# The last convolution on 32x32 tiles of the array

## The chip, the cores and the metric

The kernel runs on one core of one Trainium2 chip. The metric is the device time of one execution in microseconds; a lower time is better. Before the change it is 6811.06 us (median of three runs, 6808.49 to 6813.17).

## What is computed

The input is eight images of 16 channels and 256 x 256 pixels in f32. Four layers follow one another, each of the form "normalise, convolve, add":

```
x = x + L0(gn(x))     # capsule convolution with routing
x = x + L1(gn(x))     # spline (KAN) convolution, 3x3
x = x + L2(gn(x))     # attention over 16x16 patches, each channel for itself
x = x + L3(gn(x))     # 3x3 convolution, 16 -> 16 channels, through the FFT
```

`gn` subtracts the mean and divides by the standard deviation of a group of two channels of one image. L3 multiplies the spectra of the padded kernel and of the image, which is a circular 3x3 convolution: an output pixel needs the nine pixels around it, and rows and columns wrap at the borders of the image. The addition of x and the normalisation are linear for given statistics, so the kernel folds both into the weights of L3: the weights are scaled by 1/std of the input channel, an identity is added to the middle tap, and the mean becomes a bias for each output channel.

## The kernel before, in words

The layers run one after the other; each leaves its result in DRAM. The change touches the end of layer 2 and all of layer 3.

Layer 2 (`layer2`, `attend`) works through 8 images x 16 channels, one call of `attend` for each. A call normalises the patches on VectorE (DVE, L1411), adds the embedding on GpSimd (POOL, L1415), forms the products of the attention on TensorE (PE, L1421 to L1448), and adds the residual on DVE (L1452): `y` holds 256 rows as 128 partitions x 2 rows. Its statistics go into `st3` (L1460, L1461), and two DMAs on the queue of SyncE (SP) write the rows to `x3` (L1464). `x3` is [H + 4, 16 channels, 256] for each image, with the first row kept for row -1 and the last three for rows 256 to 258; the nested function `wrap` copies these four rows from DRAM to DRAM with two DMAs (L1363, L1364), for an image at the third channel of the next one, for the last image at the start of layer 3. A scheduler places the instructions of all engines but SP, whose order in this layer is that of the code. At channel 6 of the last image `first3` loads two of the four pieces of image 0 into the patch buffer `pt0`, which is free by then (L1388).

Layer 3 (`layer3`) keeps the order of the code on all engines. Eight input rows by 16 channels fill the 128 partitions, and six output rows come of them, in three pairs. `fetch3` loads 11 such groups, each starting six rows after the one before, as 128 partitions x 11 rows of 1 KB in one DMA (L1474), and two GpSimd copies fill the wrapped columns (L1478, L1479). An image has four such pieces. `step` (called for three values of s) makes four column tiles at once: three row pairs of piece s and one of the last piece. A product is 128 partitions by 32 outputs (2 rows x 16 channels) by 512 columns (two groups); the three horizontal taps accumulate in PSUM `p3s` (L1532). DVE adds the bias and moves the sums to `y3` (L1544), and eight DMAs on the queue of ScalarE (ACT) write a step's `y3` to the output (L1551). `weights` makes the scaled weights of the next image on DVE (L1511). The statistics of the last image are not ready when the layer begins; their steps stand in the list `todo` (`stats3_steps`), and one of them is put behind the products of each group pair, with a PSUM buffer `p3b` of their own.

Every DMA of SP and ACT is given the next of eight semaphores in turn, and waits before its issue until the DMA that used the semaphore last has landed.

Of the kernel before, what the change touches and what calls it, by code (L numbers as in the profile page):

```python
# [18 lines left out]
P = 128  # L19
# [6 lines left out]

R3 = 6
# [81 lines left out]
def _ident3():  # L109

    a = np.zeros((R3 + 2, C, 3, R3 // 2, C, 2), np.float32)
    for c in range(C):
        for r in range(R3):
            a[r + 1, c, 1, r // 2, c, r % 2] = 1.0
    return a.reshape(P, 3 * C * R3)

# [15 lines left out]
def _layout(w0, bw, sw, sc, bias, wq, bq, wk, bk, wv, bv, w3):  # L132
# [28 lines left out]

    l3 = np.zeros((R3 + 2, C, 3, R3 // 2, C, 2), np.float32)
    for dh in range(3):
        for dw in range(3):
            for ro in range(R3):
                l3[ro + dh, :, dw, ro // 2, :, ro % 2] = w3[:, :, 2 - dh, 2 - dw].T
    l3 = l3.reshape(P, 3 * C * R3)
# [110 lines left out]
class _Net:  # L278
    def __init__(self, ctx, tc, d, out):
# [19 lines left out]
        self.x3 = [self.dram.tile([H + 4, C, W], F32, name=f"x3_{b}") for b in range(B)]  # L299
# [929 lines left out]
    def stats3_steps(self, pool, name, bank):  # L1229
# [31 lines left out]
        def sums():  # L1261

            for q in range(4):
                for dw in range(3):
                    nc.tensor.matmul(z()[32 * q : 32 * q + 32, :8], self.w3[:, dw, 0], nm, start=dw == 0, stop=dw == 2)
# [33 lines left out]
    def early3(self, pool):  # L1299

        self.st3 = pool.tile([P, P, 6], F32, name="st3"), pool.tile([P, 2, P], F32, name="mv3")
        self.nc.vector.memset(self.st3[1], 0.0)
        self.w3 = pool.tile([P, 3, R3 // 2, 32], F32, name="w3")
        self.nc.sync.dma_start(out=self.w3.rearrange("p d t m -> p (d t m)"), in_=self.d["l3"])
        self.small = pool
# [8 lines left out]
    def layer2(self, images=range(B), channels=range(C)):  # L1314
# [3 lines left out]
        with ExitStack() as st:  # L1318
# [43 lines left out]
            def wrap(b):  # L1362
                nc.sync.dma_start(out=self.x3[b][0:1], in_=self.x3[b][H : H + 1])  # L1363
                nc.sync.dma_start(out=self.x3[b][H + 1 : H + 4], in_=self.x3[b][1:4])  # L1364


            pts, ress = {images[0]: self.pt[images[0] % 2]}, {(images[0], 0): first}
            with tc.manual_schedule(engines={mybir.EngineType.SP}):
                for n, b in enumerate(images):
                    after = images[n + 1] if n + 1 < len(images) else None  # L1370
                    for c in channels:
                        if c == 1:
                            ress[b, 1] = rows(b, 8)
                        if c == 2 and n:
                            wrap(images[n - 1])
# [16 lines left out]
                self.wrap = lambda: wrap(images[-1])  # L1392

    def first3(self, b):

        self.x3s = {}
        at = self.pt[0].rearrange("p h c r f -> p (h c r f)")
        for i, n in enumerate((R3 // 2, 0)):
            xs = at[:, i * 4096 : i * 4096 + 11 * WP].rearrange("p (g w) -> p g w", w=WP)
            self.x3s[n] = self.fetch3(b, n, xs)  # L1400
# [7 lines left out]
    def attend(self, mid, psum, b, c, pt, res, emb, wqk, wv, bqk, bv, bc, stats):  # L1408
# [37 lines left out]
        for o in range(2):  # L1446
# [4 lines left out]
        y = mid.tile([P, 2, 16, 16], F32, name="y2", bufs=3)  # L1451
        nc.vector.tensor_tensor(  # L1452
            y,
# [4 lines left out]
        y = y.rearrange("p o n j -> p o (n j)")  # L1458
        i = b * C + c
        nc.vector.bn_stats(stats[0][:, i, :], y.rearrange("p o w -> p (o w)"))  # L1460
        nc.vector.bn_aggr(stats[1][:, :, i], stats[0][:, i])  # L1461
        rows = self.x3[b][1 : 1 + H, c].rearrange("(h k r) w -> k r h w", k=2, r=8)
        for k in range(2):
            nc.sync.dma_start(out=rows[k], in_=y[:, k])  # L1464
# [3 lines left out]
    def fetch3(self, b, n, xs):  # L1468

        nc = self.nc  # L1470
        G = 11
        g0, k = n * G, min(G, -(-H // R3) - n * G)
        at = self.x3[b][g0 * R3, 0]
        nc.sync.dma_start(  # L1474
            out=xs[:, :k, 1 : 1 + W],
            in_=bass.AP(tensor=at.tensor, offset=at.offset, ap=[[W, P], [R3 * C * W, k], [1, W]]),
        )
        nc.gpsimd.tensor_copy(xs[:, :k, 0:1], xs[:, :k, W : W + 1])  # L1478
        nc.gpsimd.tensor_copy(xs[:, :k, WP - 1 : WP], xs[:, :k, 1:2])  # L1479
        return xs  # L1480

    def layer3(self, images=range(B)):
# [6 lines left out]
        groups, G, T = -(-H // R3), 11, R3 // 2  # L1489
        with ExitStack() as st:  # L1490
            io = st.enter_context(tc.tile_pool(name="l3_io", bufs=4))
            psum = st.enter_context(tc.tile_pool(name="l3_ps", bufs=6, space=PSUM))
            w = self.w3
            stat = dict.fromkeys(images, self.bc3)

            def bank():
                t = []

                def get():
                    if not t:  # L1500
                        t.append(psum.tile([P, 512], F32, name="p3b", tag="p3b", bufs=1))
                    return t[0]
# [3 lines left out]
            def fetch(b, n):  # L1506
                return self.fetch3(b, n, io.tile([P, G, WP], F32, name="x3s", bufs=8))

            def weights(b):
                ws = io.tile([P, 3, T, 32], F32, name="ws3", bufs=2)  # L1510
                nc.vector.scalar_tensor_tensor(  # L1511
                    ws.rearrange("p d t m -> p (d t m)"),
                    w.rearrange("p d t m -> p (d t m)"),
# [7 lines left out]
            def step(b, s, ws, xs):  # L1521

                work = [(t, s, xs[s]) for t in range(T)] + [(s, T, xs[T])]
                n = [min(G, -(-(H - 2 * t) // R3) - q * G) for t, q, _ in work]
                y = io.tile([P, G, W], F32, name="y3", bufs=3)
                for g in range(0, max(n), 2):
                    ps = psum.tile([P, 2, W], F32, name="p3s")
                    size = [min(2, k - g) for k in n]
                    for dw in range(3):
                        for q, (t, _, x) in enumerate(work):  # L1530
                            if size[q] > 0:
                                nc.tensor.matmul(  # L1532
                                    ps[32 * q : 32 * q + 32, : size[q]],
                                    ws[:, dw, t],
# [121 lines left out]
```

## Time and profile before

The profiled execution is one of its own. Times in us; shares are of the span.

| | |
|---|---|
| median of three runs | 6811.06 |
| span of the profiled execution | 6812.0 |
| first product of layer 3, start | 6449.8 |
| last product of layer 3, start | 6802.0 |
| PE busy, share | 6236.7, 92% |
| DVE busy, share | 5454.4, 80% |
| POOL busy, share | 3189.4, 47% |
| ACT busy, share | 2697.8, 40% |
| DMA packets, bytes | 451064, 811.67 MB |

The parts that the text uses are these. The page's rows of busy tenths cut the span in 40 slices; layer 3 is the last two, layer 2 about the six before them. In a line of the groups, `out<-in` are tiles of the program, `128*32` the part of the array that a product uses (rows by columns), then the shapes, the count, the busy time and the mean duration, and the idle time before the group with what ended it. In the timeline a line is a run of alike instructions: start, length, engine, line of the code, count. `PEld` is PE's loading of weights, `SPq` and `ACTq` the issue of DMAs by those engines. In the windows the busy times of the engines in a stretch of time stand side by side, then the granted clock of TensorE, the busy share of the 16 DMA engines and the bytes moved.

### The profile page before, as it was taken

The page shows a single profiled execution, that of the slowest core. Times are in us where ns is not written, and L with a number is a line of the kernel's source. Part 1 is how long each engine was busy: PE and PEld are TensorE (multiplying, and loading weights), DVE is VectorE, ACT ScalarE, POOL GpSimd, SP SyncE. Part 2 cuts the span into 40 slices and gives each one's busy share as a digit, 9 for nine tenths or more (in the row PEclk, how much of TensorE's full clock was granted, in tenths as well). Part 3 has the DMA queues.
Part 4 walks back from the last instruction along what each step waited for, and adds up shares of the span by engine and source line. Part 5 has one row for each costly group of instructions (what it writes and reads, how often), then busy time and mean ns, then how long its engine had stood idle before and what let it go on. Part 6 is the DMA issues. An engine that isn't in the chain of part 4 may idle for free. (4 is left out here: it accounts for less than half of the span.)

```text
span 6812.0 us, 105519 instructions
## 1 busy us (share of the span) xinstructions
PE 6236.7 (92%) x43144; PEld 2778.8 (41%) x43144; DVE 5454.4 (80%) x6462; ACT 2697.8 (40%) x3834; POOL 3189.4 (47%) x1885
## 2 busy tenths in 40 slices
PE   3899889899888998989986999999999999999999
PEld 1333333333333333333332444444444666666633
DVE  5799999999999999999997999999999433333322
ACT  1333333333333333333332888888888222112100
POOL 0566666666666666666666344444443111111100
PEclk9999999999999999999996999999999999999999
DMA  6233333333333333333332555555556434332376
GB/s 256 60 86 95 94 87 93 93 87 87 87 87 87 93 93 90 91 90 91 87 87 72 184 174 176 176 175 175 175 177 188 121 93 102 83 93 80 98 225 181
DMA packets 451064, 811.67 MB, mean 119 GB/s; under 512 B 57490, under 2 KB 299282, under 8 KB 415378
## 3 DMA queue, kind: packets, MB, share of 16 engines
q1 hardware_dynamic: 380946, 737.52, 36.6%
q10 hardware_dynamic: 69632, 67.39, 3.4%
q8 instruction: 339, 5.55, 0.3%
q14 instruction: 147, 1.20, 0.1%
HBM read 594.31 MB, written 211.03 MB: 118 GB/s over the span
## 5 line engine op out<-in xcount | busy, mean ns | idle before, releaser
L744 POOL TENSOR_TENSOR dd<-dd 128x1024 f32<-128x1024 f32 x512 | 1213.8, 2371 | 617.6 <-DVE dd L735 597.5
L1000 PE MATMUL ps<-bases,tw 128*32 128x512 f32 (+1 forms) x13824 | 1361.2, 546 | 16.1 <-POOL bases L969 6.6
L735 DVE SCALAR_TENSOR_TENSOR dd<-rb,v 128x1024 f32<-128x1024 f32 (+1 forms) x1024 | 1066.9, 1083 | 98.6 <-PE rb L724 93.1
L969 POOL TENSOR_TENSOR bases<-e,a 128x1024 f32<-128x1024 f32 (+1 forms) x264 | 621.5, 2377 | 927.6 <-DVE e L967 927.3
L623 DVE TENSOR_TENSOR pr<-v,fb 128x2048 f32<-128x2048 f32 (+1 forms) x512 | 1011.5, 2017 | 24.2 <-PE pl L633 12.8
L517 PE MATMUL cv<-kt,w 128*128 128x512 f32 x2048 | 1000.5, 611 | 27.7 <-DVE dd L735 21.5
L526 ACT COPY v<-cv 128x1024 f32<-128x1024 f32 x512 | 517.1, 1010 | 1152.4 <-PE cv L521 1152.4
L1000 PEld LDWEIGHTS ps<-bases,tw 128*32 128x32 f32 x13824 | 596.2, 109 | 802.5 <-issue 484.8
L744 POOL TENSOR_TENSOR s<-s,dd 128x512 f32<-128x512 f32 x512 | 670.5, 1310 | 35.1
L724 PE MATMUL rb<-rs,ct_fold 32*128 32x512 f32 x3584 | 609.5, 650 | 71.3 <-ACT rs L706 67.9
L633 PE MATMUL pl<-pr,ct_fold 128*32 128x512 f32 x3584 | 533.1, 607 | 120.2 <-DVE pr L623 120.2
L744 POOL TENSOR_TENSOR s<-v,dd 128x512 f32<-128x512 f32 x256 | 330.0, 1289 | 664.9 <-DVE dd L735 664.9
L1415 POOL TENSOR_TENSOR t<-t,emb 128x512 f32<-128x512 f32 x128 | 162.0, 1266 | 962.1 <-DVE t L1411 948.2
L521 PE MATMUL cv<-kt,w 64*128 64x512 f32 x2048 | 579.0, 641 | 0.0
L517 PEld LDWEIGHTS cv<-kt,w 128*128 128x128 f32 x2048 | 354.6, 190 | 525.5 <-issue 300.5
L1421 PE MATMUL pqk<-w_qk,t 128*128 128x512 f32 x1024 | 483.5, 595 | 4.6 <-POOL t L1415 4.6
L1432 ACT ACTIVATE vt<-pv,w_b2v 128x128 f32<-128x128 f32 x512 | 146.1, 367 | 842.3 <-PE pv L1428 842.3
L1452 DVE TENSOR_TENSOR y<-po,res 128x512 f32<-128x512 f32 x128 | 88.5, 691 | 486.8 <-PE po L1448 486.8
L977 DVE SCALAR_TENSOR_TENSOR bases<-xr,xm,bases 128x1024 f32<-128x1024 f32 (+1 forms) x264 | 447.7, 1734 | 0.3 <-POOL bases L969 0.3
L954 ACT ACTIVATE sq<-a 128x1024 f32<-128x1024 f32 (+1 forms) x264 | 263.7, 999 | 231.3 <-DVE a L946 230.5
L724 PEld LDWEIGHTS rb<-rs,ct_fold 32*128 32x128 f32 x3584 | 173.2, 185 | 415.3 <-issue 220.8
L1532 PE MATMUL p3s<-x3s,ws 128*32 128x512 f32 (+1 forms) x3114 | 327.5, 561 | 4.5 <-issue 4.5
(255 smaller groups left out, 8493.3 us busy)
## 6 DMA issues: line engine op xcount, KB each, us to landing
kt<-d SPq DMA_DIRECT2D x256, 516.0 KB
xr<-x1p SPq DMA_DIRECT2D x120, 1024.0 KB
d<-dn ACTq DMA_DIRECT2D x64, 516.0 KB
xs<-in_x_dram SPq DMA_DIRECT2D x16, 2048.0 KB
xs<-in_x_dram SPq DMA_DIRECT2D x64, 512.0 KB
res<-in_x_dram SPq DMA_DIRECT2D x64, 512.0 KB
x<-s SPq DMA_DIRECT2D x128, 256.0 KB
x1p<-s SPq DMA_DIRECT2D x128, 256.0 KB
```

The costliest lines, as they stand in the source:

```text
L517: nc.tensor.matmul(ps()[:, n], w[:, 0, j, :], t[:, a : a + 2, 0:W], start=True, stop=False)
L521: nc.tensor.matmul(ps()[:, n], w[at, 1, j, :], t[at, a : a + 2, 2 - n : 2 - n + W], start=False, stop=True)
L526: nc.scalar.copy(v[h]()[:, 4 * g : 4 * g + 4, j * W : j * W + W], ps().rearrange("p n (a w) -> p (n a) w", w=W),)
L623: nc.vector.tensor_tensor(pr()[:, :n].rearrange("p n (r w) -> p n r w", w=W), v[h]()[:, 4 * g : 4 * g + n].rearrange("p n (r w) -> p n r w ...
L633: nc.tensor.matmul(pl()[at : at + 32], sel[:, g, h, :], pr()[:, t, :], start=h == 0 and g == 0, stop=h == 1 and (g == 1 or t == 3),)
L724: nc.tensor.matmul(r()[:, n], spread[at, g, h, :], rs()[at], start=True, stop=True)
L735: nc.vector.scalar_tensor_tensor(dd()[:, :n], r()[:, :n], 1.0 / B, v[h]()[:, a : a + n], ALU.subtract, ALU.mult)
L744: op("POOL", us, lambda: nc.gpsimd.tensor_tensor(out[0](), a[0](), b[0](), ALU.add), a[1] + b[1], out[1])
L969: nc.gpsimd.tensor_tensor(ring[n % 3][:, 0, p : p + m, 1 : 1 + W], rows(e), rows(a), ALU.subtract)
L977: nc.vector.scalar_tensor_tensor(r, rows(part[1]), xm[:, b : b + 1], v, ALU.is_gt, ALU.mult)
L1000: nc.tensor.matmul(out if k is None else out[:, k], lhs, rhs, start=start, stop=stop, skip_group_check=True)
L1421: nc.tensor.matmul(ps, t[:, n, k * P : (k + 1) * P], wqk[:, n, :], start=n == 0, stop=n == 1)
```

## The change

`x3` becomes [8, 16 channels, 16, 2, 258] for each image: the row modulo 8 comes first, and a row carries its wrapped columns. In `attend`, `y` has room for these two columns, two POOL copies fill them, and one DMA writes both rows of all partitions. `wrap` is gone.

In layer 3 a partition is (row mod 8, channel), and the 33 groups of 8 rows (the last is a copy of the first pair of rows) follow one another with no row loaded twice. A group of 32 partitions is a pair of rows by 16 channels. A product takes 32 partitions by 32 outputs by 512 columns, and two pairs of input rows (q = 0 and 1) x three taps make one pair of output rows. For a strip `s` of 64 output rows, the four row groups of the array write four banks of a PSUM tile and the four column groups are four runs of 16 rows; there are two such tiles, `p3`, which fill PSUM. As q = 0 and q = 1 write a bank from different row groups, ACT copies a few elements (`seen`) between them. ACT adds the bias for two banks, DVE for the other two, and the eight stores of a strip are divided between the queues of SP and ACT. Image 0 has 24 of its groups loaded in layer 2; the other nine, and three groups that the boundary between the two loads cuts, are loaded at the start of layer 3, followed by images 1 and 2. Image n + 2 is loaded after the first half of image n. The steps of the last image's statistics take a whole `p3` tile and are placed at the end of half images. The core of the diff:

```diff
-        self.x3 = [self.dram.tile([H + 4, C, W], F32, name=f"x3_{b}") for b in range(B)]
+        self.x3 = [self.dram.tile([8, C, 16, 2, WP], F32, name=f"x3_{b}") for b in range(B)]
...
 def sums():
             for q in range(4):
-                for dw in range(3):
-                    nc.tensor.matmul(z()[32 * q : 32 * q + 32, :8], self.w3[:, dw, 0], nm, start=dw == 0, stop=dw == 2)
+                at = slice(32 * q, 32 * q + 32)
+                for k in range(6):
+                    nc.tensor.matmul(
+                        z()[at, :8], self.w3[at, k // 2, k % 2], nm[at], start=k == 0, stop=k == 5
+                    )
...
 def attend(...):
-        y = mid.tile([P, 2, 16, 16], F32, name="y2", bufs=3)
+        y = mid.tile([P, 2, WP], F32, name="y2", bufs=3)
+        rows = y[:, :, 1 : 1 + W]
...
-        rows = self.x3[b][1 : 1 + H, c].rearrange("(h k r) w -> k r h w", k=2, r=8)
-        for k in range(2):
-            nc.sync.dma_start(out=rows[k], in_=y[:, k])
+        nc.gpsimd.tensor_copy(y[:, :, 0:1], y[:, :, W : W + 1])
+        nc.gpsimd.tensor_copy(y[:, :, WP - 1 : WP], y[:, :, 1:2])
+        nc.sync.dma_start(out=self.x3[b][:, c].rearrange("r h k w -> r h (k w)"), in_=y.rearrange("p k w -> p (k w)"))
...
+    def fetch3(self, b, g, n, xs):
+        rows = self.x3[b].rearrange("r c h k w -> (r c) (h k w)")
+        at = xs.rearrange("p g w -> p (g w)")
+        for k in range(g, g + n, 8):
+            m = min(8, g + n - k)
+            if k < 32:
+                self.nc.sync.dma_start(
+                    out=at[:, (k - g) * WP : (k - g + m) * WP], in_=rows[:, k * WP : (k + m) * WP]
+                )
+            else:
+                self.nc.sync.dma_start(out=at[0:32, (k - g) * WP : (k - g + 1) * WP], in_=rows[0:32, 0:WP])
...
+            def products(s, q, ws, xs, ps):
+                for dw in range(3):
+                    for j in range(4):
+                        k = (j + q) % 4
+                        for c in range(4):
+                            g = 8 * s + 2 * c + (j + q) // 4
+                            nc.tensor.matmul(
+                                ps[32 * c : 32 * c + 32, j].rearrange("p (g w) -> p g w", w=W),
+                                ws[32 * k : 32 * k + 32, dw, q],
+                                xs(k, g)[:, :, dw : dw + W],
+                                start=q == 0 and dw == 0,
+                                stop=q == 1 and dw == 2,
+                                skip_group_check=True,
+                            )
+            def finish(b, s, ps):
+                y = io.tile([P, 2, 4, W], F32, name="y3", bufs=3)
+                bias = stat[b][1][:, b : b + 1]
+                src = ps.rearrange("p j (g w) -> p g j w", w=W)
+                nc.scalar.activation(y[:, :, 0:2], src[:, :, 0:2], AF.Identity, bias=bias)
+                nc.vector.tensor_scalar(y[:, :, 2:4], src[:, :, 2:4], bias, None, ALU.add)
+                for c in range(4):
+                    for ro in range(2):
+                        row = 64 * s + 16 * c + 1 + ro
+                        n = 8 if row + 14 < H else 7
+                        yc = y[32 * c : 32 * c + 32].rearrange("(o r) g j w -> r o (g j) w", r=2)[ro]
+                        for first, m, at in ((0, n, row),) if n == 8 else ((0, 7, row), (7, 1, 0)):
+                            to = self.out[b, 0, at]
+                            (nc.scalar if c % 2 else nc.sync).dma_start(
+                                out=bass.AP(tensor=to.tensor, offset=to.offset, ap=[[H * W, C], [2 * W, m], [1, W]]),
+                                in_=yc[:, first : first + m],
+                            )
...
             with tc.manual_schedule():
+                for b in images[1:3]:
+                    xs[b] = fetch(b)
+                for n, b in enumerate(images):
+                    for s in (0, 2):
+                        ps = [psum.tile([P, 4, 512], F32, name="p3") for _ in range(2)]
+                        for q in range(2):
+                            for k in range(2):
+                                products(s + k, q, ws, xs[b], ps[k])
+                                if q:
+                                    finish(b, s + k, ps[k])
+                                else:
+                                    nc.scalar.copy(seen, ps[k][:, :, 0])
+                        if todo:
+                            todo.pop(0)[2]()
+                        while todo and todo[0][0] != "PE":
+                            todo.pop(0)[2]()
+                        if s == 0 and n + 1 < len(images):
+                            if n and n + 2 < len(images):
+                                xs[images[n + 2]] = fetch(images[n + 2])
+                            ws_after = weights(images[n + 1])
+                    if n + 1 < len(images):
+                        ws = ws_after
```

## The prediction

> **What bounds the kernel now.** The busy row of the page comes first, then the stage that the change rewrites, in windows (columns: window, its length, busy time and count of PE, PE's weight loads, DVE, ACT, POOL, then granted clock, share of the DMA engines, GB/s).
>
> ```profile
> PE   3899889899888998989986999999999999999999
> DMA  6233333333333333333332555555556434332376
> ```
>
> ```profile
> 6200.00:6300.00 100.00, 100.00 (x367) 68.51 (x366) 36.89 (x67) 20.84 (x60) 15.18 (x12) 1.00 0.29 76
> 6449.78:6804.00 354.22, 346.67 (x3348) 140.83 (x3348) 105.35 (x178) 2.97 (x4) 10.30 (x60) 0.99 0.74 212
> ```
>
> Layer 2 (first line) is PE alone. Layer 3 (second) is PE too, 347 of 354 us, with the DMA engines at 0.74. Its groups by form, and then its timeline, show how PE's time is made:
>
> ```profile
> L1532 PE MATMUL p3s<-x3s,ws 128*32 128x512 f32 x2658 | 306.7, 592 | 4.5 <-issue 4.5
> L1544 DVE TENSOR_SCALAR y<-p3s,g3a_bias 128x512 f32<-128x512 f32 x98 | 69.0, 746 | 205.2 <-PE p3s L1532 104.7 <-DMA out_dram<-y 100.5
> ```
>
> ```profile
> 6610.10 0.16 PEld L1532 LDWEIGHTS p3s<-x3s,ws 128*32 128x32 f32 x4 [0.27 <-issue]
> 6610.53 0.16 PEld L1532 LDWEIGHTS p3s<-x3s,ws 128*32 128x32 f32 x4 [0.27 <-issue]
> ...
> 6802.98 5.65 ACTq L1551 DMA_DIRECT2D out_dram<-y  x8
> ```
>
> Four products of 128x32 run together and a new four starts every 0.429 us. The records are twice the matmuls of the code (3312 for 1656): an f32 product is two passes. 3312/4 x 0.429 us is 355 us; some are half as wide, hence 347. DVE waits for PE and for stores; stores cost ACT 0.58 to 0.85 us of issue each, 0.71 on average (last line), but ACT does nothing else here. From the first product (6449.8) to the last landing (6810.9) the stage takes 361 us; the profiled execution has 6812.0, 0.9 over the median.
>
> **What the Trainium skill says.** TensorE: Matmul & The Clock Gate, Part 3: products that use different 32x32 parts of the array run together; with 16 of them at 512 columns it gives 10.6 times the speed of one after the other. No run here shows 16. The nearest is layer 1's silu products, 64x32, eight tiles, with the same step:
>
> ```profile
> 4059.67 0.15 PEld L1000 LDWEIGHTS ps<-silu,wm 64*32 64x32 f32 x8 [0.28 <-issue]
> 4060.10 0.15 PEld L1000 LDWEIGHTS ps<-silu,wm 64*32 64x32 f32 x8 [0.28 <-issue]
> ```
>
> So a doubling of the tiles in flight cost nothing there. TensorEngine Tiling (Array Packing), PSUM Bottleneck, warns that evacuation may become the limit once TensorE is faster; the trace before does not show it (ACT 3 us of 354), and I forecast it. Matmul & The Clock Gate, Part 1, has the clock halved after some 3.4 us of idle; the trace agrees: idle for 5.05 us before 6449.78, granted 0.50 from 6450 to 6455. DMA: Bandwidth & Descriptors (Issuing engines are not separate DMA queues): a second issuing engine saves only issue time; before, ACT alone issues stores, so no run shows the split.
>
> **Part by part.**
>
> *Products.* Per image 4 strips x 2 (q) x 3 (dw) x 16 = 384 matmuls of 512 columns, 3072 in all, 6144 passes. At 16 in flight one call of `products` (48) is 96/16 x 0.429 = 2.57 us, a half image (two strips, four calls) 10.3, all 16 halves 165 us. Bounds: 8 in flight doubles it, 4 makes it four times that. I take 16: eight showed no loss, and eight pairs of load and product were issued in 0.05 us.
>
> *DMA.* Out: 32768 rows of 1 KB; where several stores were queued a row took 47 ns of an engine (6638 to 6642 us), 32768 x 47/16 = 96 us. In: 7 images of 4.26 MB and 1.5 MB of the first, at about 400 GB/s (428 for 16 KB rows, 20 to 60 us; 350 to 376 for 1 KB rows here): 78 us. Sum 174 us; before, eight rows were loaded for six. So neither PE nor DMA needs more than about 175 us.
>
> *ACT's queue.* Here I see the new bound. In the program as built, ACT has for each half: evacuate half of strip 0, issue four stores, evacuate half of strip 1, issue four stores, copy `seen` twice. DVE's half of a strip waits for ACT's half (both write interleaved pieces of one `y`), the stores wait for DVE, and ACT's next evacuation stands behind its stores. Durations: ACT 128x1024 from PSUM 1.01 us (L526 copy); DVE 746 ns at 512 and 476 at 256, so 1.29 at 1024; an issue of 128 rows 0.57 plus 0.05 (layer 2's stores: two in 1.19). A strip is 1.01 + 1.29 + 4 x 0.62 + 0.1 for handing over = 4.9, two 9.8. Then `seen` of the next half's first strip, 0.25, which PE must have before it starts q=1; then q=1 itself, 2.57 + 0.35 for weight load, drain and signal; then ACT again. Period 13.0 us against PE's 10.3. The next half's q=0 lies beside the stores. First evacuation 8.0 us after the first product, 15 periods: 8.0 + 195 = 203.
>
> *Loads on the same eight semaphores.* Every DMA of SP and ACT takes the next of eight and waits for the one that held it. A 1 MB load of 8 KB rows landed 5.2 us after issue in layer 1, and follows a queued one by 2.6 (1.06 MB at 400 GB/s). At the start 10 MB go ahead of the first stores; ACT's fourth waits for the fourth load of image 2, at 26.5 us in place of 12.2: +14.3. In images 1 to 5 a load of 4.26 MB is issued after the first half (from 10.3 us behind that half's first evacuation; fourth piece lands at 23.4). ACT's fourth store of the next half then ends at 24.0, not 18.3: 5 x 5.7 = 28.5. Behind that store stand ACT's next evacuation, DVE's, and so PE; on SP only the other stores of the strip.
>
> *Statistics.* The six PE steps now take a whole p3 buffer of two, so the next half's first products wait for the last strip's evacuation: 2.5 each, two of them inside a load's wait: 4 x 2.5 = 10.
>
> *Small.* One image border store more per image, 7 x 0.62, two ACT table loads (1.28 each), mostly under the wait: 5 together. Each of the six long waits leaves PE idle 8 us; it resumes at half clock for 3.4 to 6.8 us, 2.5 lost each, and shorter gaps add some 3: 18. End: from the last q=1 to the last landing 4.9 + 1.0 + 1.3 + five issues + 2.6 to 3.4 landing, 13.1.
>
> *Layer 2.* Stores become one DMA of 2 KB rows for two of 1 KB (0.6 us of SP's queue less) behind two POOL copies (0.2 us each by L1478). POOL's next `t` waits for DVE's `t` until about 4 us after y is written, so these are covered; if not, 0.4 x 128 = 51 us is the cost. The two wrap DMAs and the column copies after each load go; both lay beside PE: nothing. First product of layer 3 as before (the last store has one DMA less, POOL's copies more). Cost 0, bounds 0 and +10.
>
> Sum: 203 + 14.3 + 28.5 + 10 + 5 + 18 + 13.1 = 291.9 us for 361.1. 6812.0 - 69.2 = 6742.8; less 0.9 to the median, 6742.
>
> **Rivals.**
> *A. The queue doesn't pace.* If ACT's issues overlap its evacuations, DMA (174 us) and PE (165) are left: with opening and last stores about 200 us, 6650. For: ACT idles now. Against: issues and evacuations stand in one queue.
> *B. Eight tiles in flight.* A call takes 5.15 us, a half 20.6, more than ACT's chain, whose load waits then vanish: 15.8 + 309 + 6.5 + 15.7 = 347, 6797. For: the trace shows no more than eight; instructions must come at 13.4 ns each and the longest dense stretch ran at 27.
> *C. Slower.* Row groups of 32 don't run together, or issue limits them: PE needs 64 calls and some 11 us, so above 5.47 us a call, below 7.5 tiles in flight, it is slower than the 361 us; at four in flight 670 us, 7120. For: products of q=0 and q=1 write a bank from different row groups. Against: silu's two row groups.
> That the change doesn't do what it says: the program as built holds 3072 products of 32x32, so no.
>
> **How the numbers follow.** Forecast 0.76, A 0.12, B 0.08, C 0.04. The forecast's own bounds: no clock loss, loads 3 us each, statistics half: 6701; issues at 0.71 and slower landings: 6775. The range reaches A and B, 6650 to 6797. A difference of 0.2% (14 us) is about what this measurement can tell from none: B ends on that line. Faster 0.91 (forecast, A, part of B), same 0.04, slower 0.05.
>
> **What would show it.** Right: layer 3 near 290 us; PE busy under 70% of it; six waits of PE of 8 us or more, in the first six images, at half clock after; a half without load near 13 us; 16 loads of weights in each 0.43 us. Wrong: a half at 10.3 us (then A), weight loads in eights (B), fours (C), or layer 2's stretch longer than before.

## The result and the profile after

The changed kernel takes 6792.66 us (median of six runs, 6788.71 to 6795.17), the kernel before in the same measurement 6810.53 (six runs, 6808.49 to 6818.89). The ratio is 0.9971, 95% interval 0.9959 to 0.9982: 18 us faster, where 69 were forecast.

The busy rows of the changed kernel's page come first. They answer to PE's and DMA's rows before; ACT's is the third.

```profile
PE   3899889899898999899886999999999999999977
ACT  1333333333333333333331888888888222112211
DMA  6233333333333333333331555555556433433266
```

The last two slices, layer 3, have PE at 7 where it was at 9, and ACT at 1 where it was idle. The windows of the same two stretches as before, layer 2 and then layer 3 from its first product to the end of the span:

```profile
6200.00:6300.00 100.00, 100.00 (x370) 69.09 (x369) 37.56 (x68) 20.25 (x59) 18.37 (x34) 1.00 0.33 80
6452.79:6792.40 339.61, 245.46 (x6204) 133.90 (x6204) 46.21 (x58) 43.69 (x68) 0.00 (x0) 0.84 0.65 194
```

Layer 2 is as it was. Layer 3 takes 339.6 us by this measure, for 362.2 before (6449.8 to 6812.0). PE is busy for 245 of them, at a mean clock of 0.84 (0.99 before). So PE has stopped being the bound, as forecast, but no engine has taken its place: ACT and DVE are busy for 44 and 46 us and the DMA engines for 0.65. The groups by form of this stretch:

```profile
L1521 PE MATMUL p<-x3s,ws 32*32 32x512 f32 x5376 | 211.4, 668 | 66.4 <-DVE y L1536 44.5 <-issue 12.0 <-DVE g3b_m L1175 4.9
L1536 DVE TENSOR_SCALAR y<-p,g3a_bias 128x1024 f32<-128x1024 f32 x28 | 35.9, 1284 | 249.3 <-ACT y L1535 215.6 <-DMA out_dram<-y 33.7
L1535 ACT ACTIVATE y<-p,g3a_bias 128x1024 f32<-128x1024 f32 x28 | 31.2, 1114 | 150.3 <-DMA out_dram<-y 99.8 <-PE p L1521 50.5
```

Read from below: ACT waits for 100 us behind stores (`out_dram<-y`), DVE for 216 us for ACT, PE for 45 us and more for DVE. That is the chain of the forecast. One round of it stands in the timeline, a half image without statistics and without a load's wait, and the start of the next half:

```profile
6645.08 1.11 ACT L1535 ACTIVATE y<-p,g3a_bias 128x1024 f32<-128x1024 f32 x1 [2.96 <-PE p L1521]
6646.23 1.28 DVE L1536 TENSOR_SCALAR y<-p,g3a_bias 128x1024 f32<-128x1024 f32 x1 [10.43 <-ACT y L1535]
6647.54 9.14 SPq L1544 DMA_DIRECT2D out_dram<-y  x8
6647.54 3.49 ACTq L1544 DMA_DIRECT2D out_dram<-y  x4
...
6651.07 1.11 ACT L1535 ACTIVATE y<-p,g3a_bias 128x1024 f32<-128x1024 f32 x1 [4.88 <-DMA out_dram<-y]
...
6653.54 3.59 ACTq L1544 DMA_DIRECT2D out_dram<-y  x4
...
6657.16 0.35 ACT L1580 COPY seen<-p 128x4 f32<-128x4 f32 x2 [4.98 <-PE p L1521]
...
6660.82 1.11 ACT L1535 ACTIVATE y<-p,g3a_bias 128x1024 f32<-128x1024 f32 x1 [3.30 <-PE p L1521]
...
6663.29 10.72 ACTq L1544 DMA_DIRECT2D out_dram<-y  x4
...
6674.05 1.11 ACT L1535 ACTIVATE y<-p,g3a_bias 128x1024 f32<-128x1024 f32 x1 [12.12 <-DMA out_dram<-y]
```

Evacuate, DVE, four issues; the same again; `seen`; q = 1. From 6645.08 to 6660.82 this is 15.74 us; 13.0 were forecast. Four issues on ACT take 3.49 and 3.59 us, 0.88 each where 0.62 was taken. The next four take 10.72, because they stand behind a load that began on SP at 6656.78.

The starts of ACT's first evacuation of each half image are these distances apart, from the first half on: 28.8, 20.5, 22.7, 20.9, 23.6, 20.8, 15.7, 25.3, 15.7, 25.0, 15.8, 25.1, 15.7, 16.8, 16.7. The first six hold a statistics step each, the three of 25 a load's wait.

### The profile page after: what moved, and what is told of

Same layout as the page of the kernel before. It is cut to its first block, busy times and chain, and to the rows that moved or that the text cites. A ratio compares the mean times of both kernels' runs of the same rounds, so it can differ in the third digit from the quotient of the medians.

```text
span 6792.4 us, 111546 instructions
## 1 busy us (share of the span) xinstructions
PE 6136.1 (90%) x46024; PEld 2773.5 (41%) x46024; DVE 5395.3 (79%) x6342; ACT 2738.6 (40%) x3898; POOL 3219.0 (47%) x2077
## 5 line engine op out<-in xcount | busy, mean ns | idle before, releaser
L1001 PE MATMUL ps<-bases,tw 128*32 128x512 f32 (+1 forms) x13824 | 1361.3, 546 | 16.4 <-POOL bases L970 6.6
L624 DVE TENSOR_TENSOR pr<-v,fb 128x2048 f32<-128x2048 f32 (+1 forms) x512 | 1011.5, 2017 | 24.3 <-PE pl L634 12.9
L937 ACT ACTIVATE d<-xr,bd,sd 128x1024 f32<-128x1024 f32 (+1 forms) x264 | 319.1, 1209 | 15.7 <-DMA xr<-x1p 15.7
```

The lines of the kernel that those rows point to most:

```text
L624: nc.vector.tensor_tensor(pr()[:, :n].rearrange("p n (r w) -> p n r w", w=W), v[h]()[:, 4 * g : 4 * g + n].rearrange("p n (r w) -> p n r w ...
L1001: nc.tensor.matmul(out if k is None else out[:, k], lhs, rhs, start=start, stop=stop, skip_group_check=True)
```

## The experiments

Some words first: a call of `products` is 48 products, 96 passes; a half image is four calls, for two strips; to evacuate is to add the bias and move a strip from PSUM to `y3`; a stand of PE is idle time for which the profile shows nothing that it waits for.

The theory is that of the forecast, with new prices: ACT's queue paces, and behind it stands PE, for which a weight load with its pass takes 33 ns (96 of a call in 3.17 us) and not 26.8, since, as I took it, instructions reach it no faster. Rival 1 is that PE with its restarts sets the pace by itself, rival 2 that the transfer of the stores does. Layer 3 starts between 6448 and 6461 us in these runs, as the layers ahead vary from run to run, so the table gives the length of layer 3 in the profiled execution too, from its first product to the end of the span. Beside these runs the kernel before took 6812.7 to 6815.0 us at the median, so a difference of some 4 us between medians of the table says little.

| run | median us | ratio to before, 95% | layer 3 |
|---|---|---|---|
| before | 6810.5 | | 362.2 |
| after | 6792.7 | 0.9971, 0.9959 to 0.9982 | 339.6 |
| e1 stores on SP | 6744.7 | 0.9899, 0.9884 to 0.9914 | 290.0 |
| e2 parts of y apart | 6794.5 | 0.9974, 0.9962 to 0.9985 | 338.1 |
| e3 no statistics | 6782.0 | 0.9955, 0.9941 to 0.9970 | 329.8 |
| e4 no loads | 6766.3 | 0.9931, 0.9915 to 0.9948 | 311.1 |
| e5 half of the stores | 6772.7 | 0.9939, 0.9924 to 0.9954 | 318.9 |
| e6 a strip an engine | 6752.7 | 0.9911, 0.9896 to 0.9926 | 299.5 |
| e7 PE alone | 6677.5 | 0.9799, 0.9784 to 0.9813 | 224.4 |
| e8 PE alone, 256 columns | 6657.4 | 0.9770, 0.9753 to 0.9786 | 204.9 |
| e9 statistics' place | 6780.7 | 0.9952, 0.9937 to 0.9967 | 330.4 |
| e10 loads spread | 6775.4 | 0.9944, 0.9930 to 0.9959 | 322.6 |
| e11 all together | 6710.2 | 0.9849, 0.9832 to 0.9865 | 254.9 |
| e12 rows of 64 | 7324.9 | 1.0751, 1.0735 to 1.0767 | 871.8 |
| e13 rows of 1 KB | 6720.5 | 0.9859, 0.9842 to 0.9875 | 262.6 |
| e14 together, no loads | 6681.3 | 0.9807, 0.9792 to 0.9822 | 227.4 |

### e1: all stores on SP

```diff
-                            (nc.scalar if c % 2 else nc.sync).dma_start(
+                            nc.sync.dma_start(
```

> All eight stores of a strip go to SP's queue, ACT only evacuates. Theory (ACT's queue paces: evacuate 1.11, DVE's part 1.28 behind it, four issues 3.5, evacuate, DVE, four issues, then `seen` and the q = 1 products): ACT no longer stands behind stores, so PE's supply of products is next, four calls of 3.17 us. A half image without statistics falls from 15.7 to 12.7 us, one with a statistics step from 20.7 to 17.9, the 9.4 us of a load wait fall to the 2.4 us for which PE itself stands during a load. Layer 3 takes 263 us for 338: 6718 us. Rival 1 (PE with its restarts at half clock paces by itself): gain under 15 us, 6778 or more. Rival 2 (the transfer of the stores paces, whoever issues them): 6790 or more.

Both rivals fall: 48 us less. Half images without statistics and without a load's wait take 12.7 to 13.0 us, four calls of 3.17. Those with statistics take 15.4 to 18.8. What the expectation had wrong is the load's wait: three halves still take 21.8 to 25.4. It has only moved. SP's own stores now stand behind the loads' semaphores, the three buffers of `y3` run full, and then ACT's evacuation waits, as the timeline of this run shows (12.67 us):

```profile
6616.12 1.11 ACT L1535 ACTIVATE y<-p,g3a_bias 128x1024 f32<-128x1024 f32 x1 [12.67 <-DMA out_dram<-y]
6627.74 1.11 ACT L1535 ACTIVATE y<-p,g3a_bias 128x1024 f32<-128x1024 f32 x1 [2.96 <-PE p L1521]
6630.91 1.11 ACT L1535 ACTIVATE y<-p,g3a_bias 128x1024 f32<-128x1024 f32 x1 [2.06 <-PE p L1521]
```

The last two lines are the free run: two evacuations 3.17 us apart, both waiting for PE alone.

### e2: the parts of y apart

```diff
-                nc.scalar.activation(y[:, :, 0:2], src[:, :, 0:2], AF.Identity, bias=bias)
-                nc.vector.tensor_scalar(y[:, :, 2:4], src[:, :, 2:4], bias, None, ALU.add)
+                nc.scalar.activation(y[:, 0], src[:, 0], AF.Identity, bias=bias)
+                nc.vector.tensor_scalar(y[:, 1], src[:, 1], bias, None, ALU.add)
```

> ACT and DVE take one group of each bank in place of two banks each, so that their parts of y are apart and DVE does not wait for ACT. Theory: each strip of the chain through ACT's queue is shorter by about 1.15 us, 2.3 us in each of the 15.5 half images, so 36 us less: 6757 us. Rivals 1 and 2 (PE's own pace; the transfer of the stores): under 5 us less. If ACT and DVE slow each other down on a bank of PSUM that both read, the gain is smaller and their durations show it (1.11 and 1.28 us now).

Inconclusive, since the edit didn't take the wait away: in the program as built DVE waits for ACT still, and in the trace it starts 1.15 us after ACT, as before. Both now read the same banks, so my account of that wait (interleaved pieces of one `y`) is at least not the only reason for it. e6 puts the question in another way.

### e3: no statistics

```diff
-            stat[images[-1]], todo = self.stats3_steps(self.small, "g3b", bank)
+            todo = []
```

> Leaves out the statistics steps of the last image, which takes those of the others. Theory: a statistics step makes PE wait for the evacuation of the strip before, so that nothing of the next half lies beside the stores: six half images take 20.7 us in place of 15.7, 30 us in all. Without them the load waits of images 1 and 2, which the slow halves hide now, come back with about 7 us each: 6776 us. Rival (the statistics lie beside the wait for ACT's queue and cost nothing): within 5 us of 6793.

Ten us less in layer 3, as the theory has it, and by its two parts: halves that held a step fall from 20.7 to 16.4 to 17.3 us, and five halves take 24.2 to 24.6, one for each load, where there were three of 25.

### e4: no loads

```diff
-                                xs[images[n + 2]] = fetch(images[n + 2])
+                                xs[images[n + 2]] = xs[images[1 + (n + 1) % 2]]
```

> Leaves out the loads of images 3 to 7, which are computed from the tiles of images 1 and 2. Theory: ACT's fourth store waits for a load's semaphore; three half images lose 9.4 us by it, and two lose 2.6 us in which PE stands during the load: 33 us less, 6760 us; every half image from the seventh on takes 15.7 us. Rival (the wait is for the stores' own transfers, or PE's pace): under 10 us less.

26 us less, for 33: no half of 25 us is left, but those from the seventh on take 15.8 or 16.7 to 18.1, not 15.7. The longer ones hold a call whose weight loads take 3.2 to 4.1 us from first to last, for 2.4, after PE's wait of some 3 us ahead of the second strip. A wait of this length sometimes halves the clock and sometimes doesn't.

### e5: half of the stores left out

```diff
+                            if c % 2 == 0:
+                                continue
-                            (nc.scalar if c % 2 else nc.sync).dma_start(
+                            nc.scalar.dma_start(
```

> Leaves out the four stores of each strip that SP issues; ACT's stay where they are. Theory (ACT's issues are dear, 0.88 us, because SP issues at the same time; one queue alone takes 0.60 us): ACT's four take 2.5 us in place of 3.5, a half image without statistics or load wait falls from 15.7 to 13.7, and a load wait is shorter because half as many stores stand behind the loads' semaphores. In all 48 us less: 6745 us. Rival (ACT's issue price is its own, 0.88, whoever else issues): a half image stays at 15.7 us, and only load waits shrink: 6770 us.

The price is as the theory has it. ACT's four issues without SP's beside them, in the timeline of this run:

```profile
6710.69 2.56 ACTq L1546 DMA_DIRECT2D out_dram<-y  x4
```

That is 0.64 with the gaps; the median issue is 0.61 us, for 0.88 with SP beside it, and for 0.60 of SP's when it alone issues all (e1). Half of the transfers are gone too, but in e1, with all of them, an issue takes no more. Half images take 14.2 to 14.4 us, for 15.7: some 1.4 us less, where eight cheaper issues alone would give 2.1. The time as a whole is the rival's, for another reason: the load waits did not shrink (24.5 to 27.7 us for three halves), as SP, free of stores, now issues the loads earlier, between ACT's stores.

### e6: each strip evacuated by one engine

```diff
-                nc.scalar.activation(y[:, :, 0:2], src[:, :, 0:2], AF.Identity, bias=bias)
-                nc.vector.tensor_scalar(y[:, :, 2:4], src[:, :, 2:4], bias, None, ALU.add)
+                if s % 2:
+                    nc.vector.tensor_scalar(y, src, bias, None, ALU.add)
+                else:
+                    nc.scalar.activation(y, src, AF.Identity, bias=bias)
```

> ACT evacuates all four banks of the even strips, DVE all of the odd ones, so that DVE's part neither waits for ACT's nor stands behind ACT's stores. Stores as they were. Theory: ACT's round is evacuate 2.1, four issues 3.5, four issues 3.5, `seen` 0.2, then q = 1 with 3.3, 12.7 to 13.2 us in place of 15.7; a half with statistics 16.6 in place of 20.7; load waits stay at about 9 us. 49 us less: 6744 us. Rival 1 (PE's pace with its restarts) and rival 2 (the transfer of the stores): within 10 us of 6793.

40 us less with the same products, and the same stores on the same queues: rivals 1 and 2 fall here too. Halves of 13.5 to 14.4 us, three of 23.6 to 26.9 with a load's wait. ACT's `seen` is still late behind eight issues of both strips, as the timeline of this run has them:

```profile
6628.33 8.28 ACTq L1546 DMA_DIRECT2D out_dram<-y  x8
```

### e7 and e8: PE alone

Evacuation and stores of all halves but the last go, and the statistics and later loads as in e3 and e4:

```diff
-                                if q:
+                                if q and full:
                                     finish(b, s + k, ps[k])
```

In e8 each product takes `[:, :1]` of the two groups besides.

> Leaves out evacuation and stores of all half images but the last (ACT copies 4 elements per bank in their place), the statistics steps, and the loads of images 3 to 7: products alone, 512 columns each. Theory: PE cannot be given pairs of weight load and product faster than one in 33 ns when none are in store, so a call of 96 takes 3.17 us and a half image 12.7: 6676 us. Rival (16 tiles step at the 0.429 us that eight tiles showed, 26.8 ns a pair): a half image of 10.3 us, 6639 us.

> As the run with products alone, but with 256 columns in each product (half of the pixels are left out), the last half image apart. Theory (the supply of instructions sets the 33 ns): a call still takes 3.17 us, 6676 us as with 512 columns. Rival (the stream of columns through the array sets it): a call takes about 1.6 us, a half image 6.4, 6577 us.

The windows of the two runs over the same 60 us, e7 first:

```profile
6560.00:6620.00 60.00, 60.00 (x1831) 42.02 (x1816) 1.26 (x3) 3.08 (x19) 0.00 (x0) 1.00 0.02 4
```

```profile
6560.00:6620.00 60.00, 47.07 (x2063) 32.28 (x2077) 0.84 (x2) 3.58 (x22) 0.00 (x0) 1.00 0.02 4
```

1816 weight loads in 60 us are 33.0 ns each, 12.7 us a half image, and 6677.5 for 6676 expected: the pace is PE's own. But its reason was wrong. With half of the columns 2077 come in the 60 us, 28.9 ns each, which fits neither side, and PE is busy for only 47 of them. The timeline of PE in e8 shows why:

```profile
6548.87 3.11 PE L1521 MATMUL p<-x3s,ws 32*32 32x256 f32 x127 [0.98 <-issue]
6552.44 2.96 PE L1521 MATMUL p<-x3s,ws 32*32 32x256 f32 x128 [0.46 <-issue]
6556.19 2.77 PE L1521 MATMUL p<-x3s,ws 32*32 32x256 f32 x128 [0.79 <-issue]
6559.93 3.11 PE L1521 MATMUL p<-x3s,ws 32*32 32x256 f32 x128 [0.97 <-issue]
```

PE works in batches of 128 and stands between them with nothing waited for. A batch comes each 3.74 us, 29.2 ns a pass. In the same 60 us the DMA view has one kind of traffic only, the instructions:

```profile
q8 instruction: 16, 0.26, 1.8%
```

That is 16 packets of 16 KB, one in 3.75 us, so a batch is a packet. The times of the packets in the trace show it too: in these 60 us PE begins a batch 1.2 to 1.5 us after a packet has ended, each time. The Trainium skill (Runtime: NRT & Kernel Launch, Instruction fetch mechanics) has the same block of 16 KiB, 256 instructions, and calls its cost "mostly hidden"; here it isn't. In e8 the supply of instructions is the bound, and the profile can show it. Inside a batch 32 passes (both of 16 products) take 0.62 us by the starts of the records, in e7 1.06. The difference, 0.44, is twice the 0.21 us that 256 columns take less. So with 512 columns the columns set the pace, with 0.2 us more in each 32 passes than the 0.86 of the forecast: a tile's second pass starts 0.43 us after its first, its next first pass 0.64 after that. The supply lies close behind, 29.2 ns for 33.0.

### e9: the statistics in another place

```diff
-                        t.append(psum.tile([P, 4, 512], F32, name="p3"))
-                    return t[0][:, 0]
+                        t.append(held[0][:, 3])
+                    return t[0]
...
+                                if todo and not q and not k:
+                                    held[:] = [ps[1]]
+                                    todo.pop(0)[2]()
```

> The statistics steps use one bank of the second PSUM tile of a half before its products are written there, in place of a PSUM tile of their own between two halves. Nothing is left out. Theory: the cost of a step is the PSUM tile, for which the next half waits until the last strip is evacuated; with it gone the six slow halves fall from 20.7 to 15.7 us, and the load waits of images 1 and 2, which they hid, come back as in the run without statistics: 6780 us. Rival (the steps' own work costs): within 4 us of 6793.

The time is as expected, and layer 3 the same as without the steps (330.4 and 329.8): the work of the steps costs next to nothing; their PSUM tile, with its place between two halves, does. The edit moves both, so the two are not told apart. The parts came less well: halves with a step but no load's wait take 17.4 to 19.6 us, not 15.7, and later ones without a wait 15.7 to 16.9.

### e10: the loads in two parts

```diff
-                            if n and n + 2 < len(images):
-                                xs[images[n + 2]] = fetch(images[n + 2])
+                        if n and n + 2 < len(images):
+                            xs[images[n + 2]] = fetch(images[n + 2], slice(0, 2) if s == 0 else slice(2, 5))
```

> The five pieces of a load are issued as two after the first half of an image and three after the second. Theory (a store stands in ACT's queue until a load that used its semaphore has landed): six semaphores stay free for ACT's and SP's next stores, and two or three pieces land before the seventh store; a load wait falls from 9.4 to 0 to 2 us, 28 us less: 6764 us. Rival (the wait is for room on the DMA engines, however the loads are cut): within 8 us of 6793.

17 us less, between the two. The wait itself goes as the theory has it: ACT's second evacuation follows its first by 6.5 to 6.9 us in the late images; in the changed kernel it is 6.0 without a load and 13.2 to 13.6 with one. But every half with a piece of a load is longer than one without, by other ways: two halves with their pieces take 33.7 us (17.5 and 16.2), for 40.8 before the edit and 31.5 without a load.

### e11, e13 and e14: all together

e6, e9 and e10 in one, with the even strips stored by ACT and the odd ones by SP, so that one strip's issues come from one queue, and with the loads issued after the first strip of a half image:

```diff
-                            (nc.scalar if c % 2 else nc.sync).dma_start(
+                            (nc.sync if s % 2 else nc.scalar).dma_start(
...
-                for b in images[1:3]:
+                for b in images[1:2]:
                     xs[b] = fetch(b)
```

> All together: ACT evacuates and stores the even strips, DVE evacuates and SP stores the odd ones, statistics in a bank of the half's second tile, loads in two and three pieces, image 2 not loaded ahead. Theory: PE's supply, 12.7 us a half image, is all that is left besides the opening (18 us for the first half), PE's standing during loads (about 10 in all) and the end (13): 228 us for layer 3, 6681 us. Rival (transfers: 174 us by their rates, with stores and loads at the same time): halves of 14 us or more, 6700 and up.

This version is the fastest that computes all, 6710 us, 1.5% under the kernel before (1.35 to 1.68). It misses the expectation by 29 us, though: late halves with a piece of a load take 15.2 to 16.9 us, those without (the last three) 12.7 to 12.9. In the timeline of PE it stands in them after 128 passes, or 256, as in e8, though each has 512 columns here:

```profile
6569.53 4.91 PE L1526 MATMUL p<-x3s,ws 32*32 32x512 f32 x128 [0.40 <-issue]
...
6581.42 4.50 PE L1526 MATMUL p<-x3s,ws 32*32 32x512 f32 x128 [1.92 <-issue]
6586.42 9.35 PE L1526 MATMUL p<-x3s,ws 32*32 32x512 f32 x256 [0.50 <-issue]
```

e14 leaves the later loads out of e11; e13 keeps them and sets the rows of the tile 8 bytes apart, so that a load moves rows of 1 KB.

```diff
-                xs = tiles[b] if b in tiles else io.tile([P, 33, WP], F32, name="x3s", bufs=3)
+                xs = tiles[b] if b in tiles else io.tile([P, 33, WP + 2], F32, name="x3s", bufs=3)[:, :, :WP]
```

> As the run with all together, without the loads of images 3 to 7 (computed from the tiles of images 1 and 2). Theory: what is above PE's 12.7 us a half comes from the loads alone; all halves from the fourth on take 12.7 to 13.0: L3 of 220 to 226 us for 255, 6678 us. Rival (evacuation, stores and `seen` still cost in each half): halves of 14 us or more, 6695.

> As the run with all together, but a row of the loaded images stands apart in the tile, so that a load of images moves rows of 1 KB in place of 8 KB. Theory (PE's instructions come through the same DMA engines, and wait there behind the long rows of a load; a half with a load takes 16.2 us for 12.7): with short rows they wait less, a half with a load takes 13 to 14.5 us: about 6685 us. Rival (the DMA engines have no room for both, 0.87 busy): no gain, 6710 us or more, since short rows move more slowly.

Over the same 60 us, e11 and then e14:

```profile
6560.00:6620.00 60.00, 51.77 (x1433) 28.76 (x1408) 10.05 (x6) 7.22 (x11) 0.00 (x0) 1.00 0.88 280
```

```profile
6560.00:6620.00 60.00, 60.00 (x1831) 44.11 (x1816) 12.40 (x7) 11.14 (x13) 0.00 (x0) 1.00 0.63 163
```

Without loads PE gets its 1816 weight loads, the number of PE alone, with all evacuations and stores beside it: these and `seen` then cost nothing, and the statistics little (layer 3 is 227.4 us, for 224.4 without them in e7). With loads it gets 1408, 11 batches of 128: a batch of instructions takes 5.5 us in place of the 3.74 it can come in. PE's idle time in this window, 8.2 us, is all put down to `issue`, and each stand of 0.9 us or more in it ends 1.2 to 1.5 us after a packet of instructions has ended, as in e8. So the loads hold up PE's instructions; in all they cost e11 27 us. In the changed kernel the same shows as the stands of 2.4 and 2.9 us in two halves (1.4 us after a packet there too). Short rows don't help (262.6 for 254.9), so my account of the length of their rows falls. A packet itself takes no longer with loads (median of 1.0 us in e8 and in e11): it begins later, every 3.4 to 7.3 us in e11 for 3.4 to 4.1 in e8. What it waits for before it begins, with the DMA engines 0.88 busy in e11 and 0.87 with short rows over the same 60 us, stays open.

### e12: rows of 64

In e11, for the two of four output pairs with both input pairs in the same 64 partitions:

```diff
-                    for j in range(4):
+                    for j in range(4)[q :: q + 1]:
...
-                                ws[32 * k : 32 * k + 32, dw, q],
-                                xs(k, g)[:, :, dw : dw + W],
+                                wp[32 * k : 32 * k + 64, dw] if two else ws[32 * k : 32 * k + 32, dw, q],
+                                xs(k, g, 64 if two else 32)[:, :, dw : dw + W],
```

> As the run with all together, but the two of four output pairs whose input pairs lie in the same 64 partitions are made in one product of 64x32 each, so that a strip takes 72 products in place of 96. Theory (the supply of instructions sets PE's pace, 33 ns a pair): 9.5 us a half image, so that the transfers are next with about 11: 201 us for layer 3, 6655 us. Rival (the array sets it; a 64x32 product takes the room of two): no change against the run with all together, 6681 us.

A plain miss: 510 us slower than the kernel before in the same measurement (6814.6), and it says nothing about the supply. Its timeline has one j after the other:

```profile
6849.60 1.93 PE L1532 MATMUL p<-x3s,wp 64*32 64x512 f32 x8
6851.46 0.19 PEld L1532 LDWEIGHTS p<-x3s,ws 32*32 32x32 f32 x8 [1.66 <-issue]
6851.46 1.93 PE L1532 MATMUL p<-x3s,ws 32*32 32x512 f32 x8
...
6873.78 7.26 PE L1532 MATMUL p<-x3s,ws 32*32 32x512 f32 x70
```

Eight passes, the four column groups of one j, take 1.86 us, at a granted clock of 0.50 in the whole stretch though PE is busy: four in flight and no more. Shared rows are not what it comes of: j = 1 on rows 32 to 63 and j = 2 on rows 64 to 127 share none, and that step takes 1.86 us as well. In the last line (from its ninth pass on q = 1) all products have 32 rows, and a new eight starts about every 0.85 us at the same clock; products of 64x32 alone ran eight at a time in layer 1. So the loss goes with the change of height from one j to the next. Why such a change costs this, and why the clock stays at 0.50, isn't shown.

## Why the forecast was wrong

The mechanism was right in the main. The bound moved from PE to ACT's queue with the order that was forecast (e1 and e6 show it, with the same products and stores), and A, B and C were not it: halves are far from 10.3 us, and 33 ns a pass are 13 weight loads in 0.43 us, not 16, and not eight or four. B's 6797 us lies near the measurement by chance. But no sign of being right came at its number: layer 3 takes 340 us and not 290, PE is busy for 72% of it, just over the 70 that were named, a half without a load takes 15.7 us, and of PE's waits only one is over 8 us (11.3; the next are 7.3 and 6.6). What failed is the size of the terms. Forecast and measurement, with the distances listed above:

| term | forecast | measured |
|---|---|---|
| first evacuation after the first product | 8.0 | 14.0 |
| 15 rounds of a half image | 195 (13.0) | 236 (15.73) |
| opening loads | 14.3 | 8.1 (28.8 - 20.7) |
| load waits | 28.5 | 33 (3 x 9.4, 2.0 and 2.8) |
| statistics | 10 | 30 (6 x (20.7 - 15.7)) |
| small, half clock | 23 | 2, the rest in the rows above |
| end, to the last landing | 13.1 | 15.4 |
| sum | 291.9 | 338.5 |

With 3.0 us for a later first product (below) the difference is 49.6 us, and 6742 + 49.6 = 6792.

*The step that failed first is the price of an issue in "ACT's queue".* It took 0.62 us from layer 2, where SP issues alone, for stores that both queues issue at the same time. Side by side they take 0.88 at the median on ACT, the first of four 0.59 and the others mostly 0.86 to 1.0: by the chain 8 x 0.26 x 15 = 31 us of the 49.6 (e5's halves, 1.4 us shorter, would make it 21). It is no wait for a semaphore: in the first two rounds of stores shown above (from 6647.54 and 6653.54) the semaphore of every store was free 0.8 us or more before its issue. e1 and e5 show the price of one queue alone (0.60, 0.61) and what it buys. The prediction saw that no run showed the split, and it had 0.71 for the last eight of ACT's own stores in the profile before, but it kept that for the upper bound only (6775), which was still short. (The median of all 192 there, issued by ACT alone, is 0.62: it is the crowd that costs, rather than ACT. Why it does isn't shown; in e11 and e14, where the issues of the two queues meet only in part, ACT's beside SP's take 0.62 and 0.72 at the median.) The Trainium skill's sentence (DMA: Bandwidth & Descriptors, Issuing engines are not separate DMA queues), that a second engine saves issue time only, agrees: eight stores are issued in 3.5 us from two queues, in 5.1 from one. That the time of each rises is not in it.

*Statistics.* The place and the wait were right, the size not. A step was costed as one evacuation, 2.5 us, but PE also starts cold after it: its next call runs at half clock, with 4.13 us from the first weight load to the last (2.4 to 2.8 elsewhere), and q = 0 of both strips no longer lies beside the stores. That makes 5.0 a step, clock included. e3 and e9 show that this is the PSUM tile, or its place, and not the work.

*Products.* 16 in flight were right; "eight showed no loss" was carried over to 16 at the same step, 0.86 us for 32 passes. It is 1.06 (e7, e8). The skill's 10.6 for 16 tiles, which the prediction quoted and didn't use, spoke for a loss: against one pass in each 0.429 us, 96 in 3.17 us are 13.0 times. It cost little here (3.44 us from q = 1 to the evacuation where 2.92 was taken, 8 us in all), because PE had slack; it is the bound of e14.

*Load waits.* Semaphores and places were right, in three halves of five; in the other two the statistics hid the wait, and PE's standing during loads took its place, a term the prediction had not. 9.4 for 5.7 comes of the landing: the fourth piece lands 16.6 us after the first is issued (6656.78 to 6673.40), 13.1 were taken, as stores are under way at the same time. The opening is shorter than forecast since the first evacuation is later, behind calls at half clock and one stand of PE (2.1 us).

*Layer 2.* The cost of 0 was right for the stretch; 3.0 us came at its end. The last `y` is written 2.25 us later than before, 0.7 of it from ahead of layer 2. Its store leaves behind two POOL copies and lands 4.1 us after issue (2.7 before), and the first weights of layer 3 wait for that:

```profile
6448.10 0.57 SPq L1458 DMA_DIRECT2D x<-y  x1
6452.30 0.42 DVE L1504 SCALAR_TENSOR_TENSOR ws<-w,g3a_bc,ct_ident 128x192 f32<-128x192 f32 x1 [3.65 <-DMA x<-y]
```

Most of the stage's gain on paper, 362 us against the 227 of e14, went into the turn that ACT's queue takes for each strip, and then into the loads.

## What to carry over

When the bound goes from an engine to a queue, price every instruction of that queue as it will run there, with the other queues issuing beside it, and put the price of the crowd into the range. Put evacuations, stores and the small copies that the matmuls wait for on different queues, or in an order in which none stands behind another's waits, before a faster matmul is expected to pay. A borrowed PSUM buffer or semaphore can cost more than the work that borrowed it.

## What the hardware showed besides

- A store's issue of 128 rows of 1 KB took 0.60 us on SP (e1) or 0.61 on ACT (e5) alone, and 0.88 on ACT when both queues issued four at the same time (changed kernel); medians all.
- With 16 tiles of 32x32 in flight 32 f32 passes of 512 columns took 1.06 us, of 256 columns 0.62.
- PE's instructions come in packets of 16 KB, 128 weight loads with their passes, one in 3.74 us in e8 and in some 5.5 us while loads run (e11). PE then stands without a semaphore in sight, until 1.2 to 1.5 us after a packet has ended.
- Products of 64x32 and 32x32 in turn ran four at a time, whether they shared rows or not (eight passes in 1.86 us, e12), and the granted clock stayed at 0.50 for the 872 us of that layer though PE was busy.
